# Layers 2 and 3 of a sparse graph stack: from a scheduler's order to one written by hand, with powers on GpSimd, W3 loaded in layer 1 and matrix products that nobody reads

## Chip, cores and metric

One core of one Trainium2 chip. The metric is the device time of one execution in microseconds: 997.93 us, the median of three runs (997.87 to 998.99). The profile comes from a fourth execution with the recorder on, which took 1028.73 us.

## What is computed

A stack of four graph layers on x (2708 nodes, 512 features, float32) with one weighted adjacency matrix adj (2708 x 2708, some 4 entries off the diagonal in a row). Each layer is added to its input and normalised over the features:

```python
x = ln(x + (x - (adj @ x) * (diag + 1)) @ weight + bias)                    # layer 0
# layer 1: h = x @ W_sa; attention e = exp(-leaky_relu(s_left + s_right)) where adj != 0
x = ln(x + sigmoid(gate_a * (e / e.sum(1)) @ h + gate_b * (adj @ (x @ W_gcnb) + b_gcnb)))
head = (adj > 0) / maximum(sqrt((adj > 0).sum(1)), 1e-12)                   # layer 2
inc = adj + head
x = ln(x + (inc @ x) / inc.sum(1))
A = adj + eye; d = A.sum(0) ** -0.5                                         # layer 3
x = ln(x + tanh((d[:, None] * A * d[None, :] @ x) @ W.T + b))
```

## The kernel before

**Blocks.** The rows are cut into NB = 24 blocks of R = 113 (the last has 109). In layer 0 each block's rows of adj are searched for their largest entries (`find`: `max` and `max_index` on four segments, L837 and L838), and the list of edges of a block is packed into EC = 4 chunks of 128. From there on a product with adj is sparse: `gather` (L613) fetches the source rows of a block's edges from a table in device memory with four indirect DMAs, issued by POOL, one per chunk of 128 rows; `values` (L1220) builds on DVE the 128 x 113 selection matrix of each chunk with the edges' values; `aggregate` (L626) multiplies the two on PE, eight passes of 128x512 a block (four products in float32, two passes each). There are NGB = 3 buffers for gathered rows, so gathers can run two blocks ahead. A gather for a layer can start only when all rows of its table have been stored (`move_rows`, L567, on SP's queue), since an edge may point to any row.

**Order.** Layers 0 and 1 are issued under a manual schedule (`by_hand`, entered at L656, closed after layer 1): the order of the code is the order on each engine. Layer 0 has a prologue (L1079 to L1160), in which the first blocks' searches, the loads of weights and the first products are interleaved by hand, and a loop over k = 1 to 23 (L1163), in which PE does for each block `o_l` (projection, L582), `h` and `hb` (the projections for layer 1) and `l0a` (aggregation). Layer 1's loop (L1465) has for each block the gathers of 4116-byte rows, two aggregations (`l1s`, `l1e`), the gates, a tanh, the statistics (`stats1`, whose add and power run on POOL, L1428 and L1429), and `norm1`, which stores the new x to table[1].

After the manual schedule is closed, the degrees go through device memory and back in another layout (L1501 to L1511), the row norms, row sums and d are computed for all blocks at once in [128 x 24] tiles (L1515 to L1547, square roots on ACT at L1523 and L1541), and layers 2 and 3 run through `run_layer` (L1234): for each block a gather two ahead, `prepare` one ahead, `compute`, and `finish` of the block before. Here a scheduler decides the order on each engine. Layer 2's `l2_prepare` turns the row norm into a row (`spread`: transpose on PE L1229, copy on ACT L1231) and makes the incidence (`inc`, L1564 and L1567, on DVE); at block 3 it issues the loads of b3 (to all 128 partitions) and W3 (1 MB). `l2_finish` has the node's own part on ACT (L1577), the sum on DVE (L1578), the `layernorm` (L591: statistics on DVE, square root on ACT L598, reciprocal and shift on DVE L599 and L601, scaling on ACT L604), and y = x d (L1583) to table[2]. Layer 3 aggregates again (`l3a`), adds the own part (`l3u`, L1599), transposes and projects with W3 (`tr_l` L573, `uT_l` L575, `o_l` L582), adds the bias (L1604), takes a tanh on ACT (L1607), adds x (L1608), normalises and stores.

The last lines of layer 1 and the two functions that set layers 2's and 3's order in the code are shown here with the rest that the diff touches.

Of the kernel before, what the change touches and what calls it, by code (L numbers as in the profile page):

```python
# [447 lines left out]
def sparse_stack(  # L448
# [142 lines left out]
    def layernorm(dst, v, r, name, scale=None, dst2=None):  # L591

        stats = small.tile([P, 6], FP, tag="stats", name=f"st_{name}")
        nc.vector.bn_stats(stats[:r, :], v)  # L594
        mv = small.tile([P, 2], FP, tag="mv", name=f"mv_{name}")
        nc.vector.bn_aggr(mv[:r, :], stats[:r, :])
        rstd = small.tile([P, 1], FP, tag="rstd", name=f"rs_{name}")
        nc.scalar.activation(rstd[:r, :], mv[:r, 1:2], AF.Sqrt, bias=eps_ln[:r, :])  # L598
        nc.vector.reciprocal(rstd[:r, :], rstd[:r, :])  # L599
        shift = small.tile([P, 1], FP, tag="shift", name=f"sh_{name}")  # L600
        nc.vector.tensor_scalar(  # L601
            shift[:r, :], mv[:r, 0:1], rstd[:r, :], -1.0, op0=ALU.mult, op1=ALU.mult
        )
        nc.scalar.activation(dst, v, AF.Identity, bias=shift[:r, :], scale=rstd[:r, :])  # L604

# [51 lines left out]
    with ExitStack() as phase:  # L657
# [117 lines left out]
        def spread_rows():  # L775
            for t in (ndiag, b0_bc):
                o = ps_o.tile([P, D], FP, tag="o", name="over_rows")
                nc.tensor.matmul(o, lhsT=one_row, rhs=t[0:1, :], start=True, stop=True)
                nc.scalar.copy(t, o)
            nc.vector.tensor_scalar(ndiag, ndiag, -1.0, -1.0, op0=ALU.mult, op1=ALU.add)  # L780
# [34 lines left out]

        def score_columns():
            w_a = work.tile([P, D], FP, tag="v", name="w_a_rows")
            nc.scalar.copy(w_a[0:2, :], w_saT["sum"][0:2, :])
            ps = ps_tr.tile([P, DB, P], FP, tag="tr", name="w_a_t")
            for f in range(DB):  # L820
                nc.tensor.transpose(ps[:, f, 0:2], w_a[0:2, f * P : (f + 1) * P], ident[0:2, 0:2])
            nc.scalar.copy(w_sa_sb[:, :, D : D + 2], ps[:, :, 0:2])
# [7 lines left out]
        def find(i, parts=range(NG)):  # L830

            a = abuf[i % NA]
            for g in parts:
# [3 lines left out]
                nc.vector.max(out=top, in_=seg)  # L837
                nc.vector.max_index(  # L838
                    out=where_all[:, i, g * 8 : (g + 1) * 8], in_max=top, in_values=seg
                )  # L840
# [237 lines left out]

        clear_diagonal(0)  # L1079
        negatives(0)  # L1080
        find(0)
        clear_diagonal(1)
        negatives(1)
        count(0)
        starts(0)
        find(1, (0,))
        ranges(0)
        nc.scalar.memzero(gflat[1])
        nc.scalar.memzero(gflat[2][:, KB * R + 3 * D :])
        mark(0)  # L1090
        fetch(0)
        find(1, (1,))
# [7 lines left out]
        w_gc_sb = load_w(w_gc, "w_gc_sb", first)  # L1100
        clear_diagonal(2)
        pick(0)
        values0(0)
        find(1, (2, 3))
        count(1)
        starts(1)
        find(2, (0,))
        ranges(1)
        negatives(2)
        mark(1)  # L1110
        spread_rows()
        fetch(1)
        find(2, (1,))
        clear_diagonal(3)
        pick(1)
        values0(1)

        nc.gpsimd.memset(abuf[4 % NA][:, NF, 0:1], 0.0)
        load_adj(4)
        sums0(0)  # L1120
        inputs0(0)
        turn_u(0)
        find(2, (2, 3))
# [4 lines left out]
        find(3, (0,))  # L1128
# [5 lines left out]
        fetch(2)  # L1134
        residual0(0)
# [6 lines left out]
        find(3, (1,))  # L1142
        norm0(0)
        values0(2)
# [3 lines left out]
        turn_u(1)  # L1148
        times_a(2)
        times_a(3)  # L1150
        score_columns()
        negatives(3)
        find(3, (2, 3))
        clear_diagonal(4)
        count(3)
        load_adj(6)
# [6 lines left out]
        for k in range(1, NB):  # L1163
            m, b = k + 2, k + 3
            if m < NB:
                starts(m)
                ranges(m)
            turn_x(k - 1)
            project0(k)
            if k > 1:  # L1170
                store0(k - 2)
# [3 lines left out]
            if m < NB:  # L1175
                mark(m)
                fetch(m)
# [3 lines left out]
            if b + 1 < NB:  # L1181
                clear_diagonal(b + 1)
            if m < NB:
# [3 lines left out]
            next0(k - 1)  # L1187
# [22 lines left out]
        rest0(NB - 1)  # L1210
        store0(NB - 1)
# [13 lines left out]

    def spread(col, name):

        ps = ps_s.tile([P, P], FP, tag="s", name=f"sp_{name}")
        nc.tensor.transpose(ps[:, :R], col[:R, :].to_broadcast([R, P]), ident[:R, :R])  # L1229
        row = spool.tile([P, R], FP, tag="row", name=f"row_{name}")  # L1230
        nc.scalar.copy(row, ps[:, :R])  # L1231
        return row

    def run_layer(src, n, prepare, compute, finish):  # L1234
        ahead = [gather(gath[i % NGB], i, src, n) for i in range(NGB - 1)]
        ready = prepare(0, ahead[0])
        done = None
        for i in range(NB):
            if i + NGB - 1 < NB:
                ahead.append(gather(gath[(i + NGB - 1) % NGB], i + NGB - 1, src, n))  # L1240
            ready_next = prepare(i + 1, ahead[i + 1]) if i + 1 < NB else None
            done_next = compute(i, ahead[i], ready)
            if i > 0:
                finish(i - 1, done)
            done, ready = done_next, ready_next
        finish(NB - 1, done)
# [202 lines left out]
    def spread_bias():  # L1449
        ps = ps_sp.tile([P, 4, P], FP, tag="sp", name="bg_rows")  # L1450
        ps = ps.rearrange("p k r -> p (k r)")
        nc.tensor.matmul(ps, lhsT=one_row, rhs=bg_bc[0:1, :], start=True, stop=True)
        nc.vector.tensor_copy(bg_bc, ps)
# [7 lines left out]
    spread_bias()  # L1461
    scores1(0)
    mask1(0)
    for i in range(NB):
# [9 lines left out]
        scored_sums1(i)  # L1474
        if i + 1 < NB:
# [9 lines left out]
        if i > 0:  # L1485
            norm1(i - 1)
        if i < KB:
            source_sum(i)
    both1(NB - 1)
    stats1(NB - 1)  # L1490
    norm1(NB - 1)
    phase.close()
    by_hand.close()

    ps_agg = ctx.enter_context(tc.tile_pool(name="ps_agg2", bufs=4, space=bass.MemoryType.PSUM))
    ps_tr = ctx.enter_context(tc.tile_pool(name="ps_tr2", bufs=1, space=bass.MemoryType.PSUM))
    ps_o = ctx.enter_context(tc.tile_pool(name="ps_o2", bufs=1, space=bass.MemoryType.PSUM))
    ps_s = ctx.enter_context(tc.tile_pool(name="ps_s2", bufs=2, space=bass.MemoryType.PSUM))


    deg_t = ps_s.tile([P, P], FP, tag="s", name="deg_t")  # L1501
    nc.tensor.transpose(deg_t[:KB, :], deg_k, ident)
    deg_c = gpool.tile([KB, P], FP, name="deg_c")
    nc.scalar.copy(deg_c, deg_t[:KB, :])
    nc.sync.dma_start(out=deg_d, in_=deg_c)
    flat_deg = deg_d.rearrange("b p -> (b p)")
    deg_r = gpool.tile([NB, R], FP, name="deg_r")
    nc.sync.dma_start(out=deg_r, in_=flat_deg[: NB * R].rearrange("(b p) -> b p", p=R))
    deg_s = ps_s.tile([P, P], FP, tag="s", name="deg_s")
    nc.tensor.transpose(deg_s[:R, :NB], deg_r, ident[:NB, :NB])  # L1510
    nc.scalar.copy(deg[:R, :], deg_s[:R, :NB])  # L1511

    plus = const.tile([P, NB], FP, name="plus")  # L1515
    nc.vector.tensor_scalar(plus, adiag, 0.0, None, op0=ALU.is_gt)
# [146 lines left out]
```

## Time and profile before

| What | Value |
|---|---|
| Median of three runs | 997.93 us |
| Profiled execution: time | 1028.73 us |
| Profiled execution: span from first to last instruction | 1026.9 us |
| Mean granted TensorE clock | 0.94 |
| PE busy in the span | 869.7 us (85%), 2921 instructions |
| DVE busy | 697.3 us (68%) |
| ACT busy | 598.6 us (58%) |
| POOL busy | 448.3 us (44%) |
| Moved by DMA | 190.80 MB, mean 186 GB/s |
| Layer 0 | 0 to about 428 us |
| Layer 1 (first `l1s` 442.7) | to about 650 us |
| Layer 2, first to last gather | 662.26 to 801.34 us |
| Layer 3, first gather to last product | 817.39 to 1012.7 us |

How to read it. Engines are PE (matrix products), PEld (loads of stationary operands, beside PE), DVE, ACT, POOL and SP (whose queue issues most plain DMAs). A group line names the source line, engine, operation, out<-in tiles and count, then the busy time and mean of one, and after the bar the engine's idle time before these instructions with what ended it: "<-issue" is time in which it waited for nothing that the profile shows, "<-remote" is a releaser that could not be placed. The granted clock is the share of full speed that PE's throttle allowed. The ends of matrix products are modelled in this recording, and single records can be missing.

### The profile page before, as it was taken

How to read it: one execution, taken by the hardware profiler on the slowest of the kernel's cores; microseconds unless marked ns; L12 is line 12 of the kernel's file. 1: busy time of each engine (PE TensorE's matmuls, PEld its weight loads, DVE VectorE, ACT ScalarE, POOL GpSimd, SP SyncE). 2: the span in 40 equal slices, each digit the busy share in tenths (PEclk: the TensorE clock that was granted, in tenths of full speed). 3: DMA queues.
4: the chain of work that ended last, by engine and by line, in shares of the span. 5: the costliest groups of instructions: out<-in, count | busy, mean ns of one | idle time of the engine just before them, and what ended most of it. 6: DMA issues, size and time to landing. Idle time of an engine off the chain costs nothing.

```text
span 1026.9 us, 11065 instructions
## 1 busy us (share of the span) xinstructions
PE 869.7 (85%) x2921; PEld 481.2 (47%) x2921; DVE 697.3 (68%) x1977; ACT 598.6 (58%) x1248; POOL 448.3 (44%) x492
## 2 busy tenths in 40 slices
PE   1889999999999999888888889386666568999993
PEld 1345555555555555456666667232222223444441
DVE  7778888888888873258887889645755515555553
ACT  7476676676666754357676766424433405666665
POOL 3222332323323221066666764276767275555510
PEclk9989999999999999989999999688889788999998
DMA  9856757657566334189999996276667364555521
GB/s 245 267 142 171 195 160 204 176 159 202 168 192 185 106 109 135 54 288 292 299 289 311 300 310 213 83 217 189 197 188 208 105 171 137 163 163 162 164 78 35
DMA packets 126857, 190.80 MB, mean 186 GB/s; under 512 B 81080, under 2 KB 81126, under 8 KB 126785
## 3 DMA queue, kind: packets, MB, share of 16 engines
q0 software_dynamic: 36864, 111.73, 36.5%
q1 hardware_dynamic: 89921, 78.28, 26.6%
q8 instruction: 25, 0.41, 0.2%
q14 instruction: 47, 0.39, 0.1%
HBM read 176.54 MB, written 27.80 MB: 199 GB/s over the span
## 4 chain that ended last, share of the span: by engine, by line
PE 60%; DVE 10%; DMA 10%; issue 6%; another core or an unknown queue 5%; ACT 4%; POOL 4%; SPq 0%; POOLq 0%; DVEq 0%; ACTq 0%
PE o_l L582 16%; DMA gath<-table,source 9%; PE h L582 8%; PE l0a L626 8%; PE hb L582 8%; PE l3a L626 7%; PE l2a L626 6%; POOL gath L613 3%; PE fetched L900 2%; PE tr_l L573 2%; ACT uT_l L575 1%; DVE st_l L1424 1%; DVE s L1220 1%; DVE e L1338 1%
## 5 line engine op out<-in xcount | busy, mean ns | idle before, releaser
L613 POOL DMA_INDIRECT gath<-table,source x288 | 311.3, 1081 | 200.4 <-issue 68.5
L613 POOL DMA_INDIRECT gath<-in_x_dram,source x96 | 96.8, 1008 | 261.3 <-issue 222.0
L626 PE MATMUL l2a<-gath,inc 128*113 128x512 f32 (+1 forms) x192 | 100.0, 673 | 48.7 <-DVE st_l L594 19.1
L1355 PE MATMUL l1s<-gath,s 128*113 128x256 f32 (+3 forms) x384 | 96.6, 407 | 26.9 <-DVE l1b L1385 26.4
L626 PE MATMUL l3a<-gath,s 128*113 128x512 f32 (+1 forms) x192 | 92.8, 607 | 11.4 <-DMA gath<-table,source 11.3
L582 PE MATMUL o_l<-shared,uT_l 128*113 128x512 f32 (+1 forms) x192 | 88.5, 604 | 11.3 <-issue 10.0
L1355 PEld LDWEIGHTS l1s<-gath,s 128*113 128x113 f32 (+1 forms) x384 | 70.3, 188 | 53.5 <-DVE l1b L1385 34.2
L582 PE MATMUL o_l<-w_sb,uT_l 128*113 128x512 f32 (+1 forms) x192 | 90.3, 614 | 2.2 <-ACT uT_l L575 1.1
L575 ACT COPY uT_l<-tr_l 128x452 f32<-128x452 f32 (+1 forms) x48 | 26.0, 541 | 112.3 <-PE tr_l L573 105.8
L582 PE MATMUL h<-w_sa_sb,uT_x 128*113 128x259 f32 (+1 forms) x384 | 88.3, 382 | 0.0
L626 PE MATMUL l0a<-gath,s 128*113 128x512 f32 (+1 forms) x192 | 88.2, 603 | 0.0
L1365 PE MATMUL l1e<-gath,e 128*113 128x257 f32 (+3 forms) x384 | 87.0, 379 | 0.0
L582 PE MATMUL hb<-w_gc_sb,uT_x 128*113 128x512 f32 (+1 forms) x192 | 86.6, 593 | 0.0
L626 PEld LDWEIGHTS l2a<-gath,inc 128*113 128x113 f32 (+1 forms) x192 | 36.6, 202 | 105.2 <-issue 65.7
L1365 PEld LDWEIGHTS l1e<-gath,e 128*113 128x113 f32 (+1 forms) x384 | 68.0, 177 | 15.5 <-issue 0.4
L582 PEld LDWEIGHTS h<-w_sa_sb,uT_x 128*113 128x113 f32 (+1 forms) x384 | 66.1, 177 | 15.2 <-issue 1.0
L582 PEld LDWEIGHTS o_l<-shared,uT_l 128*113 128x113 f32 (+1 forms) x192 | 32.7, 180 | 62.4 <-issue 49.2
L1599 DVE SCALAR_TENSOR_TENSOR l3u<-xr,dself,l3a 113x512 f32<-113x512 f32 (+1 forms) x24 | 17.9, 747 | 60.9 <-PE l3a L626 52.7
L1220 DVE TENSOR_SCALAR s<-niota_r,nrow,edges 128x113 f32<-128x113 f32 x192 | 58.8, 336 | 0.4 <-PE l1s L1355 0.4
L626 PEld LDWEIGHTS l3a<-gath,s 128*113 128x113 f32 (+1 forms) x192 | 32.8, 182 | 51.4 <-issue 36.5
L582 PEld LDWEIGHTS hb<-w_gc_sb,uT_x 128*113 128x113 f32 (+1 forms) x192 | 33.9, 177 | 46.5 <-issue 46.0
L582 PEld LDWEIGHTS o_l<-w_sb,uT_l 128*113 128x113 f32 (+1 forms) x192 | 32.9, 181 | 44.6 <-issue 37.5
(240 smaller groups left out, 1591.5 us busy)
## 6 DMA issues: line engine op xcount, KB each, us to landing
shared<-in_adj_dram SPq DMA_DIRECT2D x14, 1186.5 KB
table<-st SPq DMA_DIRECT2D x23, 450.2 KB
shared<-table SPq DMA_DIRECT2D x23, 448.0 KB
gath<-in_adj_dram SPq DMA_DIRECT2D x7, 1186.5 KB
xi<-in_x_dram SPq DMA_DIRECT2D x23, 224.0 KB
table<-xr SPq DMA_DIRECT2D x23, 224.0 KB
table<-y SPq DMA_DIRECT2D x23, 224.0 KB
out_dram<-y SPq DMA_DIRECT2D x23, 224.0 KB
```

The source lines that it names most:

```text
L573: nc.tensor.transpose(tr[:, f, :r], u[:r, f * P : (f + 1) * P], ident[:r, :r])
L575: nc.scalar.copy(uT[:, :, :r], tr[:, :, :r])
L582: nc.tensor.matmul(o, lhsT=uT[:, f, :r], rhs=w[:, f, :], start=(f == 0), stop=(f == DB - 1))
L613: nc.gpsimd.indirect_dma_start(out=g[:, c, :n], out_offset=None, in_=src[:, :], in_offset=bass.IndirectOffsetOnAxis(ap=source[:, i, c : c ...
L626: nc.tensor.matmul(agg[:r, :], lhsT=s[:, c, :r], rhs=g[:, c, off : off + D], start=(c == 0), stop=(c == EC - 1),)
L900: nc.tensor.matmul(t["fetched"][:, c, : 3 * NS], lhsT=t["q"][:, c * P : (c + 1) * P], rhs=rec_all[:, i].rearrange("p k s -> p (k s)"), sta ...
L1220: nc.vector.tensor_scalar(s[:, c, :], niota_r, nrow[:, i, c : c + 1], edges[:, i, c, 1:2], op0=ALU.is_equal, op1=ALU.mult,)
L1338: nc.vector.tensor_tensor(e, gath[i % NGB][:, :, SR : SR + 1].to_broadcast([P, EC, R]), over_chunks(s_left[:, i, :]), ALU.add,)
L1355: nc.tensor.matmul(sum_s[i][:r, k, : at.stop - at.start], lhsT=s[:, c, :r], rhs=g[:, c, at], start=(c == 0), stop=(c == EC - 1),)
L1365: nc.tensor.matmul(sum_e[i][:r, k, k : k + at.stop - at.start], lhsT=e[:, c, :r], rhs=g[:, c, at], start=(c == 0), stop=(c == EC - 1),)
L1424: nc.vector.bn_stats(stats[:r, :], v[:r, :])
L1599: nc.vector.scalar_tensor_tensor(u[:r, :], x3, dself[:r, i : i + 1], agg[:r, :], op0=ALU.mult, op1=ALU.add)
```

## The change

The manual schedule is no longer closed after layer 1 but at the end of the kernel. `run_layer`, `layernorm` and `spread` are gone, and layers 2 and 3 are written out in the order in which each engine is to do them. The main parts:

1. **Layer 0's prologue** is reordered: searches split into values and places, `negatives`, `clear_diagonal` and the zeroing of buffers moved later, `values0` of blocks 1 and 2 behind their neighbours' turns, the score columns split and moved into k = 1. `keep_busy(n)` issues n matrix products of 128x512 into a PSUM tile that is never read: 6 at the start, then 2, 1, and 4 ahead of layer 0's last store.
2. **Layer 1's last blocks** now hold the degrees' way out (block 22) and back (block 23), the row norms for columns 0 to 21 (block 22) and 22 to 23 (after the loop), as maximum on DVE and a power on POOL in place of square root and reciprocal, and the loads of b3 (one row, spread by a product and a copy on DVE) and W3, after block 22's norm. d is a power on POOL too. Twelve unread products (`keep_warm`) stand between the last block's products and b3's spreading.
3. **Layer 2**: turning and copying the norm two blocks ahead, the copy first on ACT; the aggregation; one unread product a block; the statistics of the block before; values two ahead; and so on, as below. The incidence has a ring of three places in memory that layer 1 used for s_left. The last two `values` of the loop are those of layer 3's blocks 0 and 1. Nine unread products follow the loop.
4. **Layer 3**: the projection is one block behind the aggregation, the tanh and the norm two behind; the statistics take add and power on POOL in place of the square root on ACT. The last block's tanh and statistics go by halves of 256 columns.

PSUM for layers 2 and 3 is laid out anew: two buffers for aggregations (four before), two for projections (one before), two for turned rows, one for transposes, one for unread products.

```diff
+        def keep_busy(n):
+
+            o = ps_o.tile([P, D], FP, tag="o", name="unread")
+            for _ in range(n):
+                nc.tensor.matmul(o, lhsT=ident, rhs=iota_t, start=True, stop=True)
...
+        keep_busy(6)
         clear_diagonal(0)
         negatives(0)
         find(0)
...
+        keep_busy(1)
         inputs0(0)
         turn_u(0)
+        values0(1)
         find(2, (2, 3))
...
-        values0(2)
         inputs0(1)
         times_a(1)
         turn_w(3)
         turn_u(1)
+        values0(2)
         times_a(2)
         times_a(3)
-        score_columns()
-        negatives(3)
-        find(3, (2, 3))
+        score_rows()
+        find(3, (1, 2, 3))
...
         for k in range(1, NB):
             m, b = k + 2, k + 3
+            if k == 1:
+                turn_x(k - 1)
+                project0(k)
             if m < NB:
                 starts(m)
+                if k == 1:
+                    score_columns()
                 ranges(m)
...
+    def keep_warm(pool, tag, shape, n, cols=D):
...
+        for _ in range(n):
+            nc.tensor.matmul(o[:, :cols], lhsT=ident, rhs=bg_bc[:, :cols], start=True, stop=True)
...
+    def row_norms(at):
...
+        nc.vector.tensor_scalar(inv_norm[:, at], cnt[:, at], 1e-24, None, op0=ALU.max)
+        nc.gpsimd.tensor_tensor(
+            inv_norm[:, at], inv_norm[:, at], root.to_broadcast([P, n]), ALU.pow
+        )
...
         scored_sums1(i)
+        if i + 1 == NB:
+            source_sums_in()
+            turn_norm(0)
+            turn_norm(1)
...
             norm1(i - 1)
+        if i + 1 == NB:
+            nc.sync.dma_start(out=b3_bc[0:1, :], in_=b3[None, :])
+            nc.sync.dma_start(out=w3_sb, in_=w3T.rearrange("(b p) o -> p b o", p=P))
         if i < KB:
             source_sum(i)
+        if i == KB:
+            source_sums_out()
+            row_norms(slice(0, KB))
+    row_norms(slice(KB, NB))
+    copy_norm(0)
+    copy_norm(1)
+    keep_warm(ps_sp, "sp", [P, 4, P], 12)
     both1(NB - 1)
     stats1(NB - 1)
-    norm1(NB - 1)
-    phase.close()
-    by_hand.close()
...
-    nc.scalar.activation(inv_norm, inv_norm, AF.Sqrt)
-    nc.vector.reciprocal(inv_norm, inv_norm)
...
+    norm1(NB - 1)
...
-    nc.scalar.activation(d_inv, d_inv, AF.Sqrt)
-    nc.vector.reciprocal(d_inv, d_inv)
+    nc.gpsimd.tensor_tensor(d_inv, d_inv, root.to_broadcast([P, NB]), ALU.pow)
+    spread_bias(b3_bc)
+    phase.close()
...
+    own2(0)
+    for i in range(NB):
+        if i + 2 < NB:
+            gather(gath[(i + 2) % NGB], i + 2, table[1], D)
+            turn_norm(i + 2)
+            copy_norm(i + 2)
+        sum2[i] = aggregate(inc2.pop(i), gath[i % NGB], rows(i), f"l2a{i}")
+        if i + 1 < NB:
+            keep_warm(ps_u, "u", [P, D], 1)
+        if i > 0:
+            stats2(i - 1)
+        s = values((i + 2) % NB)
+        if i > 0:
+            norm2(i - 1)
+        if i + 1 < NB:
+            own2(i + 1)
+        if i + 2 < NB:
+            incidence(i + 2, s)
+        else:
+            edge_3[(i + 2) % NB] = s
+    stats2(NB - 1)
+    norm2(NB - 1)
...
+    keep_warm(ps_u, "u", [P, D], 9)
...
+        nc.gpsimd.tensor_scalar(mv[:r, 1:2], mv[:r, 1:2], 1e-5, None, op0=ALU.add)
+        nc.gpsimd.tensor_tensor(mv[:r, 2:3], mv[:r, 1:2], root[:r, :], ALU.pow)
...
+    for i in range(2):
+        gather(gath[i], i, table[2], D)
...
+    for i in range(NB + 1):
+        if i + 2 < NB:
+            gather(gath[(i + 2) % NGB], i + 2, table[2], D)
+        if i > 0:
+            uT = turned(u3.pop(i - 1), rows(i - 1), f"l3_{i - 1}")
+        if i < NB:
+            sum3[i] = aggregate(edge_3.pop(i), gath[i % NGB], rows(i), f"l3a{i}")
+        if i > 1:
+            tanh3(i - 2, whole)
+        if i + 2 < NB:
+            edge_3[i + 2] = values(i + 2)
+        if i > 0:
+            project3(i - 1, uT)
+        if i > 1:
+            stats3(i - 2, whole)
+        if i < NB:
+            inputs3(i)
+        if i > 1:
+            norm3(i - 2)
+    tanh3(NB - 1, two)
+    stats3(NB - 1, two)
+    norm3(NB - 1)
+    by_hand.close()
```

## Prediction

> **What bounds the kernel now.** I read the windows by stage first, then the groups, the waits of the gathering engine, and the chain across the joint of layers 2 and 3.
>
> ```profile
> 430.00:650.00 220.00, 187.09 (x799) 142.70 (x797) 175.06 (x453) 144.31 (x361) 132.44 (x142) 0.95 0.86 273
> 650.00:662.00 12.00, 2.17 (x6) 0.99 (x6) 10.09 (x42) 9.19 (x15) 1.17 (x2) 0.56 0.13 39
> 662.00:815.00 153.00, 100.77 (x210) 39.03 (x210) 85.04 (x253) 59.71 (x114) 97.71 (x96) 0.82 0.64 190
> 815.00:850.00 35.00, 18.66 (x43) 7.15 (x43) 6.54 (x15) 3.08 (x5) 24.26 (x24) 0.75 0.57 158
> 850.00:1012.00 162.00, 160.75 (x437) 68.83 (x438) 85.84 (x229) 107.58 (x133) 75.36 (x73) 0.99 0.46 137
> ```
>
> Columns: stretch and length, then busy PE, PEld, DVE, ACT, POOL, then granted clock, DMA share, GB/s. Layer 1 (430 to 650) lives on its transfers (share 0.86) and is hardly touched. Layer 3 from 850 on is PE-bound: 160.75 of 162 us. Between lie three stretches where no engine is full, at clocks of 0.56, 0.82 and 0.75.
>
> ```profile
> L613 POOL DMA_INDIRECT gath<-table,source x96 | 97.7, 1018 | 45.6 <-issue 19.8 <-remote 12.5 <-PE l2a L626 5.5
> L1578 DVE SCALAR_TENSOR_TENSOR l2v<-l2a,row_cnt,l2v 113x512 f32<-113x512 f32 (+1 forms) x24 | 18.0, 748 | 34.3 <-remote 26.0 <-PE l2a L626 6.4 <-issue 1.8
> POOL gath L613 <- DMA table<-y: 16.0, 1, 16.0
> ```
>
> A gather takes 1.02 us and about 0.29 us of issue follows, so 1.306 us each and 5.22 us a block. That is layer 2's floor: 24 x 5.22 = 125.4 us. It took 139.1 us (662.26 to 801.34): 13.7 us too long. After the last gather another 16.0 us pass before layer 3's first gather.
>
> ```profile
> 819.99 3.70 DMA gath<-table,source
> 829.12 1.10 PE l3a L626 x2
> 833.19 8.35 another core or an unknown queue
> 841.60 6.31 another core or an unknown queue
> 847.93 0.76 DVE l3u L1599
> 849.95 5.12 PE o_l L582 x8
> ```
>
> On one core "another core" cannot be meant. DVE and ACT wait there for PE's semaphore: between 831.8 and 841.5 ten passes of 128x512 took 9.7 us, where the warm L0 loop needs 0.43 each. Such joint stalls of 7 to 10 us come at 688, 714, 744, 784 and 833; a granted clock of 0.5 over 10.2 us follows each. I read them as PE running at half clock after idle stretches.
>
> ```profile
> L582 PE MATMUL o_l<-shared,uT_l 128*113 128x512 f32 (+1 forms) x183 | 84.5, 605 | 11.3 <-issue 10.0 <-ACT uT_l L575 1.2
> L598 ACT ACT_TABLE_LOAD x23 | 29.5, 1283 | 0.4
> L1607 ACT ACT_TABLE_LOAD x22 | 28.2, 1283 | 27.8 <-DVE l3v L1604 26.4 <-issue 1.4
> ```
>
> In layer 3 o_l's first start is 849.95 and its last 1009.02: 159.1/22 = 7.23 us a block. The 45 table loads (57.7 us of ACT) are beside that PE work and cost nothing, except at the end.
>
> ```profile
> 56.92 1.27 PE w_a L810 x2
> 58.22 0.58 ACT w_a_rows L818
> 58.85 0.58 PE w_a_t L821 x4
> 60.80 5.28 PE o_l L582 x8
> 66.95 3.51 PE h L582 x16
> 70.47 3.43 PE l0a L626 x8
> ```
>
> This is the chain into the L0 loop. From o_l at 78.37 on, PE takes 15.95 us a block without a hole, so what is won before it is kept.
>
> **What the Trainium skill says.** "TensorE: Matmul & The Clock Gate", What's actually happening: the array falls to half its clock after an idle window of about 3.4 us of a free-running counter, and needs a busy one to come back. The trace agrees in kind (eight passes 5.3 to 5.5 us cold, 3.5 to 3.7 warm; clock 0.5 for 10.2 us at a time). "ScalarE: Activation LUTs", Table sets: square root and tanh are of different sets, so alternating them loads a table each time; the trace has two loads a block, 1.283 us each. "GPSIMD Engine Reference", Elementwise: about 2.6 cycles per element for two inputs; no price for a power. The trace has one only at [113,1]: 0.57 us, against 0.22 for a simple scalar operation. "DMA: Bandwidth & Descriptors", Issuing engines are not separate DMA queues: queues of all engines share the same 16 DMA engines; the trace agrees: W3 and b3 (1.25 MB), issued at 661, share 662 to 669 with layer 2's first gathers, and l2a starts at 669.68.
>
> **Part by part**, in the profiled execution's own time (1028.73 us; span 1026.9, 1.8 around it). It is 30.8 us longer than the median of 997.93.
>
> *L0's prologue.* The six unread products at the start have PE to themselves. score_columns goes behind project0(1): 1.27 + 0.58 + 0.58 = 2.4 us leave the chain. values0(2), four ACT selections of 0.48 us ahead of uT's copy, goes behind turn_u: 1.9 us. o_l(1) warm instead of cold: 5.28 - 3.69 = 1.6 us. Sum -5.9. Next in line is DVE with the split searches (0.66 to 0.94 us an instruction, none removed). From -2 to -9; I take -6. The four products before the last store0 fill the hole at 428 to 442: -0.5.
>
> *Joint of layers 1 and 2.* Two square roots and their loads leave ACT: table loads at 651.46 and 654.93, and tanh's own switch at 652.99; 2 x 1.28 = 2.6 us. Against that, source_sums_in's ACT copy stands ahead of the last block's gates, waiting for PE: I take +2 us. W3 and b3 (now one row) are issued under layer 1's block 23, some 9 us earlier: 1.25 MB at the 300 GB/s of layer 1 is 4.2 us of its transfers, of which block 23's gathers are already in. First gather about 662 as now. First l2a: twelve unread products, 12 x 0.43 = 5.2 us warm or 10.3 cold, then b3's copy: about 667.5. POOL goes on meanwhile as there are three buffers, so the gain here is 0, -3 to +5. The degrees' round trip (two small DMAs on SP's queue, behind layer 1's last stores) now starts a block earlier, with the 8 us of block 23 beside its two landings of some 2 us: nothing. On that queue W3 stands ahead of xr's last store, but 9 us before it. Powers: one column is between 0.02 us (the page's rate, an estimate) and 0.35 us (0.57 - 0.22); 24 columns 1 to 8.5 us, I take 4. That for columns 0 to 22 has an 8 us block beside it. d_inv's stands on POOL ahead of layer 2's first gather; its cover is the store's landing (658.0 to 662.26, 4.2 us); at 8.5 it costs 4.3.
>
> *Layer 2.* Per block: PE 8 x 0.43 + 0.26 + one unread 0.43 = 4.1 us; DVE 85.0/24 = 3.5; ACT 59.7/24 = 2.5; all under POOL's 5.22. turn_norm and copy_norm two blocks ahead, and the copy first on ACT, break the ring l2a, inc, row_in that turned one late block into a stall. ACT's square root waits on DVE as now, with own2 and the next copy_norm behind it; these have a block of slack. PE is asked for 4.1 of 5.22 us, no idle window, so it stays warm. Of 13.7 us I give 3 back for stalls that I don't see: -11.
>
> *Joint of layers 2 and 3.* Now 801.34 to 817.39, in which l2a ends 8.7 us after the last gather. With PE one block behind: last gather landed and used after 3.2, statistics and norm 4, landing of y 3.3: 10.5 us. -5.5. Nine unread products (3.9 warm, 7.8 cold) lie wholly in this gap.
>
> *Layer 3.* Now first l3a 820.8 to last o_l 1012.7: 191.9. PE warm: 24 x 7.23 = 173.5, plus gathers setting the pace of the first three blocks, 3 x (5.22 - 3.46) = 5: 178.5. -13. The 45 loads become one; POOL takes add and power, 0.22 + 0.57 us ahead of gathers, with 7.23 - 5.22 = 2.0 us spare. *Tail:* no load, halves: -1.5.
>
> Sum: -6 - 0.5 + 0 - 11 - 5.5 - 13 - 1.5 = -37.5, so 991.2 us profiled. Times 997.93/1028.73 = 0.970: 961.5. I say **962**.
>
> **Rivals.** *A: the joint stalls are mostly an effect of recording.* The profiled run is 30.8 us longer, and records are missing where PE stalls end (o_l at 849.95 shows 3 of 8 passes); but the clock column is low there too. Then the unprofiled layer 2 is already near its floor: of 11 + 13 remain perhaps 4: -37.5 + 20 = -17.5, **981**. *B: layer 2 in its fixed order gets another bound*: each DVE wait on l2a now holds the next incidence, and each ACT wait the next own2. One exposed semaphore chain of the length of sh to xr (0.6 us) in each block gives 24 x 0.6 = 14: **976**. *C: slower.* One unread product makes PE's block 4.1 us of full clock. Where the granted clock falls under 4.1/5.22 = 0.79, PE sets layer 2's pace (now 0.82 on the mean of the stage). At half clock a block is 8.2 us, 3.0 over POOL's: 24 x 3.0 = 72, with layer 2's 11 lost: 962 + 83 = **1045**. Against it: PE would have to stay cold while 80% busy, and L0's loop shows 1.00. *D: the prologue gains nothing*, because DVE's searches set it: **968**, inside the forecast's range.
>
> **How the numbers follow.** Forecast with D: 0.60 (948 to 972); A 0.20 (974 to 988); B 0.10 (970 to 982); C 0.04; 0.06 that more is won than I see (under 948: first gathers of layer 2 earlier by the 4.2 us of landing, unread products helping layer 1's end). Range 946 to 986: it leaves out C, most of the last case, and the ends of A. A measurement here tells 0.2% (2 us) from no change. Faster by more: 0.60 + 0.20 + 0.10 + 0.06, less 0.02 that I take off A for an end at no change: 0.94. Within: these 0.02. Slower: C's 0.04.
>
> **What would show it.** Right, in the changed profile: no joint stalls of 7 us and PEclk 9 or more through layer 2; gathers of layer 2 within 129 us first to last; the wait on table<-y near 10 us; layer 3 at 7.2 us a block from its second block on; 5 table loads in all; o_l(2) near 72 us instead of 78. Wrong: a clock of 0.5 with PE busy in layer 2 (C), DVE or ACT ending POOL's waits (B), stalls vanished in the profile and a smaller gain without it (A), a power over 5 us on POOL before the first gather.

## The result

The changed kernel takes 993.63 us (median of 9 runs, 991.35 to 996.93), the kernel before 998.69 us beside it (997.31 to 1000.11): a ratio of 0.9958, 95% interval 0.9944 to 0.9973. That is 5 us faster, where 36 were forecast (997.93 to 962). The forecast of 962 and its range of 946 to 986 both miss.

The profiled execution of the changed kernel took 996.16 us (span 994.3), inside its timed runs. That of the kernel before had taken 1028.73, outside all of its own: against that one recording the change looks 32.6 us faster, and 27 of these are not there when the two are timed. This is what the study had to explain.

The same stretches as before, now of the changed kernel (columns: stretch and length, then busy PE, PEld, DVE, ACT and POOL, granted clock, DMA share, GB/s):

```profile
430.00:650.00 220.00, 187.47 (x805) 142.07 (x804) 175.93 (x452) 144.41 (x364) 136.94 (x144) 0.96 0.86 272
650.00:662.00 12.00, 12.00 (x24) 4.95 (x23) 2.66 (x13) 0.81 (x1) 8.35 (x7) 0.82 0.47 147
662.00:815.00 153.00, 134.89 (x305) 49.97 (x304) 105.44 (x289) 65.88 (x120) 109.68 (x106) 0.97 0.68 196
815.00:850.00 35.00, 35.00 (x98) 15.35 (x97) 19.89 (x49) 9.65 (x15) 28.03 (x32) 1.00 0.64 178
```

The clock stands at 0.97 and 1.00 where it stood at 0.82 and 0.75, PE is busy throughout, and POOL's idle time ahead of its gathers has fallen from 200.4 to 139.7 us. First before, then changed:

```profile
L613 POOL DMA_INDIRECT gath<-table,source x288 | 311.3, 1081 | 200.4 <-issue 68.5
L598 POOL DMA_INDIRECT gath<-table,source x288 | 314.9, 1093 | 139.7 <-issue 66.7
```

Read alone, that is the forecast come true. The trap is the other half of the comparison.

### The profile page after: what moved, and what is told of

Read it like the earlier page. It is cut to its first block, busy times and chain, and to the rows that moved or that the text cites. A ratio compares the mean times of both kernels' runs of the same rounds, so it can differ in the third digit from the quotient of the medians.

```text
span 994.3 us, 11251 instructions
## 1 busy us (share of the span) xinstructions
PE 913.7 (92%) x3037; PEld 496.8 (50%) x3037; DVE 709.1 (71%) x1956; ACT 528.3 (53%) x1174; POOL 480.1 (48%) x543
## 5 line engine op out<-in xcount | busy, mean ns | idle before, releaser
L598 POOL DMA_INDIRECT gath<-table,source x288 | 314.9, 1093 | 139.7 <-issue 66.7
L1347 PE MATMUL l1s<-gath,s 128*113 128x256 f32 (+3 forms) x384 | 94.6, 401 | 26.8 <-DVE l1b L1377 26.6
L611 PE MATMUL l2a<-gath,s_left 128*113 128x512 f32 (+1 forms) x192 | 96.5, 623 | 13.0 <-DMA gath<-table,source 10.2
L611 PE MATMUL l3a<-gath,s 128*113 128x512 f32 (+1 forms) x192 | 88.5, 603 | 3.5 <-DMA gath<-table,source 3.5
L582 PE MATMUL o_l<-shared,uT_l 128*113 128x512 f32 (+1 forms) x192 | 86.5, 593 | 0.6 <-ACT uT_l L575 0.6
L1705 ACT ACTIVATE y<-l3v,mv_l 113x512 f32<-113x512 f32 (+1 forms) x24 | 19.5, 813 | 88.0 <-DVE mv_l L1701 83.5
L611 PEld LDWEIGHTS l2a<-gath,s_left 128*113 128x113 f32 (+1 forms) x192 | 30.6, 182 | 68.6 <-DMA gath<-table,source 40.7
L611 PEld LDWEIGHTS l0a<-gath,s 128*113 128x113 f32 (+1 forms) x192 | 34.2, 179 | 38.4 <-issue 36.7
```

Of the source, the lines that this page charges most:

```text
L582: nc.tensor.matmul(o, lhsT=uT[:, f, :r], rhs=w[:, f, :], start=(f == 0), stop=(f == DB - 1))
L598: nc.gpsimd.indirect_dma_start(out=g[:, c, :n], out_offset=None, in_=src[:, :], in_offset=bass.IndirectOffsetOnAxis(ap=source[:, i, c : c ...
L611: nc.tensor.matmul(agg[:r, :], lhsT=s[:, c, :r], rhs=g[:, c, off : off + D], start=(c == 0), stop=(c == EC - 1),)
L1347: nc.tensor.matmul(sum_s[i][:r, k, : at.stop - at.start], lhsT=s[:, c, :r], rhs=g[:, c, at], start=(c == 0), stop=(c == EC - 1),)
L1705: nc.scalar.activation(y[:r, :], v[:r, :], AF.Identity, bias=mv[:r, 3:4], scale=mv[:r, 2:3])
```

## Experiments

Theory S at the outset: the joint stalls of layers 2 and 3 exist only where a recording is made, and the change has taken away something that the timed runs of before never had. Rivals: they come by chance (T), or they are in every execution and the change gives the time back elsewhere (H). Eighteen kernels ran in five groups, each group on one chip, and each on another. A "stall" or "hold-up" here is a stretch in which PE starts nothing and the other engines wait for its results.

### First group: the kernel before again, and parts of the change

x1 is the kernel before, unchanged.

> The kernel before, unchanged, recorded a second time. Theory S (the joint stalls of layers 2 and 3 exist only in a recorded execution): the recorded execution again takes 15 to 45 us more than the timed ones, and the excess lies in stalls of several us between 662 and 850; the timed runs stay at 998 +- 1. Rival T (the stalls come by chance in any execution, the first recording was an outlier): the recording takes about 998 to 1003 and shows no such stalls; then layer 2's and 3's milestones of this recording are within 3 us of those of the changed kernel, moved by what comes before them. Rival H (stalls are in every execution): recording at 1028 and the timed runs would have to hold the same stalls, so a granted clock of about 0.94 in the timed runs too.

x2 has the change's layer 0 (part 1 of the change) and nothing else of it.

> The kernel before with the change's layer 0 alone (prologue, loop at k = 1, the unread products of layer 0). Theory S: the prologue's part, read from the traces as 3.1 us at the second block's own part and 3.2 at layer 1's first product, is most of the whole gain of 5 us: 994.5 to 996 us. Rival (the prologue gain is eaten by layer 1, which is bound by transfers): 997.5 to 998.7, and the gain of the change lies behind layer 1.

x3 is the changed kernel without the unread products of layers 1 to 3:

```diff
-    keep_warm(ps_sp, "sp", [P, 4, P], 12)
...
-        if i + 1 < NB:
-            keep_warm(ps_u, "u", [P, D], 1)
...
-    keep_warm(ps_u, "u", [P, D], 9)
```

> The changed kernel without the 43 unread products of layers 1 to 3 (12 ahead of layer 2, one in each block of layer 2 but the last, 9 behind it); layer 0's stay. Theory S: gathers set layer 2's pace and the unread products neither help nor hurt by more than 3 us; 992 to 997. Rival H (they keep the clock up and so save the stalls): 1005 to 1030 timed, with a granted clock under 0.95. Rival U (they are on the path at the joints): 988 to 991.

x4 is the changed kernel with all of layer 0 as before.

> The changed kernel with the layer 0 of before. Theory S: it loses the prologue's 3 us and keeps 1 to 2 from the joint of layers 1 and 2: 996 to 997.5. Rival (all the gain is in layers 1 to 3): 993 to 994.5.

| Kernel | Median, us | Ratio to before (1021.22, 49 runs) |
|---|---|---|
| x1, before again | 1021.39 | 1.0002 (0.9981 to 1.0023) |
| x2, layer 0 alone | 1017.21 | 0.9966 (0.9944 to 0.9988) |
| x3, no unread products | 1003.85 | 0.9859 (0.9808 to 0.9910) |
| x4, layer 0 of before | 1013.67 | 0.9916 (0.9893 to 0.9939) |

x3's six executions fall into two clusters, four at 1002.4 to 1004.9 us and two at 1014.2 and 1014.3.

None of the theories had expected the first line: the kernel before itself now takes 1012 to 1029 us in every execution, timed or recorded. The recorded execution is not set apart from the timed ones (x1's, 1017.52, lies among 1015.71 to 1024.89), so S falls, and with it the reason that the prediction's rival A gave. H falls too: there are executions at 998. Something that holds for the whole group of runs decides. And x4 shows that the stalls stay in the hand-written order, with PE full of products. Its PE around 692 us (start, length, instructions, idle before them):

```profile
692.35 0.26 PE L1465 MATMUL sp_in<-ident,inv_norm 113*128 113x113 f32 x1
692.45 3.60 PE L611 MATMUL l2a<-gath,s_left 128*113 128x512 f32 x8
701.31 2.07 PE L1441 MATMUL unread<-bg_bc,ident 128*128 128x512 f32 x2 [5.27 <-remote]
703.18 0.40 PE L1465 MATMUL sp_in<-ident,inv_norm 113*128 113x113 f32 x1
```

and DVE, which waits for the sum:

```profile
694.33 0.63 DVE L1481 TENSOR_TENSOR s_left<-s_left,s 128x452 f32<-128x452 f32 x1
701.25 0.75 DVE L1582 SCALAR_TENSOR_TENSOR l2v<-l2a,row_cnt,l2v 113x512 f32<-113x512 f32 x1 [6.29 <-remote]
```

Eight passes start at their full 0.43 us, the last at 695.45, then nothing starts for 5.3 us. The unread product waits for no other engine, only for PE's own signal of the sum before it, and DVE waits for the same one: both go on at 701.25 to 701.31. The two passes after it take 1.03 us each, and the clock record has 0.5 from 698.3 for 6.8 us. The half clock follows the hold-up; it isn't its start.

Whether PE itself stood still or only its signals came late isn't shown. The recordings with hold-ups hold fewer of PE's signals than others: between 662 and 800 us, 70 in the first recording and 84 in x1, against 114 in y1 below, the same kernel. In layer 0 (60 to 430 us), where no time is lost, it is 223 and 225 against 249. So a stretch without a signal measures nothing by itself; the waits do. In the five recordings with hold-ups and unread products in layer 2 (x4, w1, w2, w3, u1), PE's wait ahead of such a product is 1.7 to 6.8 us, three to five times in layer 2 (waits under 1.5 us left out).

### Second group: a chip without hold-ups

> The kernel before once more, in another call. In the call before, every execution of it took 1012 to 1029 us, where the first timed runs took 997 to 1000. Theory C (the chip decides: on some chips PE is held up for about 3.5 us and then runs at half clock for 7 to 10 us, several times in layers 2 and 3; on others it isn't): the runs of this call are either all near 998 with no such stall in the recording, or all near 1020 with 4 to 6 of them. Rival R (recording or the moment decides, not the chip): times from 998 to 1025 mixed within this call.

> The changed kernel once more. Theory C: on a chip without the stalls 993 to 994, 5 us under before; on one with them about 1009 (the earlier 1013.7 with layer 0 of before, less the prologue's 4), 11 to 13 us under before. Rival (the changed order does away with the stalls wherever it runs): 992 to 996 on any chip.

> The kernel before with the change's layer 0 alone. In the call before it was 4.0 us faster. Theory C: layer 0 shows none of the stalls, so the same 3 to 4.5 us on any chip: on one without stalls 994 to 995, which leaves 0.5 to 1.5 us for all of layers 1 to 3.

> The changed kernel without the 43 unread products of layers 1 to 3. Theory C: on a chip without stalls they are beside the gathers and cost or win at most 2 us, 992 to 995; on one with stalls they add to PE's load and it is 5 us or more faster without them (1003.9 in the call before). Rival H (they keep the clock up): slower than the changed kernel by over 3 us on a chip without stalls.

y1 is before, y2 the changed kernel, y3 and y4 are x2 and x3 again.

| Kernel | Median, us | Ratio to before (999.33, 38 runs) |
|---|---|---|
| y1, before | 999.55 | 0.9998 (0.9982 to 1.0015) |
| y2, changed | 993.61 | 0.9938 (0.9917 to 0.9959) |
| y3, layer 0 alone | 996.35 | 0.9973 (0.9964 to 0.9983) |
| y4, no unread products | 993.68 | 0.9952 (0.9934 to 0.9970) |

Theory C (its words stand at y1) foresaw this: all runs of before lie between 995.9 and 1003.3, and no group of the study mixes, for this kernel, such times with those over 1012. But no chip was met twice, so the chip and the moment can't be told apart, and nothing is on record of what the chip's other cores did. Nor does the record name the chip of the first recording: if it was that of the three timed runs at 998, something else than the chip changed. The recording y1 is the one that the prediction would have needed, layers 2 and 3 of the kernel before with no hold-up in them:

```profile
662.00:815.00 153.00, 109.49 (x233) 37.13 (x234) 87.84 (x262) 61.39 (x116) 108.60 (x107) 0.92 0.69 205
815.00:850.00 35.00, 35.00 (x95) 14.80 (x94) 17.21 (x47) 20.46 (x26) 25.75 (x25) 1.00 0.68 196
```

POOL's waits there (total, times, longest) know no "remote", and table<-y holds it for 12.4 us instead of 16.0:

```profile
POOL gath L613 <- issue: 17.7, 58, 0.3
POOL gath L613 <- DMA table<-y: 12.4, 1, 12.4
```

The stages of three recordings, each from the start of a stage's first gather to the next mark:

| Stage, us | First recording of before | y1, before | y2, changed |
|---|---|---|---|
| Layer 0, to its last own part (`l0u` of block 23) | 408.0 | 407.8 | 405.5 |
| from there to layer 1's first gather | 27.9 | 28.2 | 27.8 |
| Layer 1, first gather to block 23's | 188.9 | 187.1 | 189.4 |
| to layer 2's first gather | 37.5 | 36.6 | 36.2 |
| Layer 2, first gather to block 23's | 132.4 | 122.5 | 124.3 |
| to layer 3's first gather | 22.8 | 17.3 | 16.8 |
| Layer 3, first gather to block 23's `l3u` | 186.0 | 174.3 | 174.2 |
| from there to the end | 23.6 | 23.4 | 21.0 |

Between the first two columns, the same kernel, lie 9.9 + 5.5 + 11.7 = 27.1 us in layers 2 and 3. The change has nearly nothing there: + 1.8 - 0.5 - 0.1. Layer 1 is bound by its transfers, and its 23 blocks take 185.0 to 189.6 us over all twenty recordings, with hold-ups in layers 2 and 3 or without, which speaks against slower transfers as their cause; y2 lies near the upper end, and its recorded execution (997.0) is the slowest of its runs.

### Third group: single steps and a combination

w1 takes layer 3's root back to ACT:

```diff
-        nc.gpsimd.tensor_scalar(mv[:r, 1:2], mv[:r, 1:2], 1e-5, None, op0=ALU.add)
-        nc.gpsimd.tensor_tensor(mv[:r, 2:3], mv[:r, 1:2], root[:r, :], ALU.pow)
+        nc.scalar.activation(mv[:r, 2:3], mv[:r, 1:2], AF.Sqrt, bias=eps_ln[:r, :])
+        nc.vector.reciprocal(mv[:r, 2:3], mv[:r, 2:3])
```

> The changed kernel with layer 3's square root back on ACT (square root and reciprocal in stats3, in place of add and power on POOL), so two table loads in each block of layer 3 again, in the hand order. The prediction's step (loads lie beside PE's work and cost only at the end): 1 to 2.5 us slower than the changed kernel, all of it after the last l3u, and l3u's pace unchanged at 7.2 us. Rival (the loads hold up DVE's in-order queue and with it the next l3u): the pace rises by 0.2 us or more, 5 us slower or worse. Times hold for a chip without stalls (changed kernel 993.6).

w2 takes d_inv's root back to ACT, behind layer 1's last norm:

```diff
-    nc.gpsimd.tensor_tensor(d_inv, d_inv, root.to_broadcast([P, NB]), ALU.pow)
+    nc.scalar.activation(d_inv, d_inv, AF.Sqrt)
+    nc.vector.reciprocal(d_inv, d_inv)
```

> The changed kernel with d_inv's root on ACT and a reciprocal on DVE, in place of the power on POOL (4.17 us on 24 columns), which in the recordings ends 0.17 us before layer 2's first gather starts. If the power sets that gather: first gather 1.0 to 1.3 us earlier against the last norm of layer 1, time 992.5 on a chip without stalls. If the landing of the last store sets it: no difference within 0.3 us there.

w3 has four more unread products in layer 0:

```diff
+                if k == 1:
+                    keep_busy(4)
                 turn_u(k + 1)
```

> The changed kernel with four more unread products in layer 0, at k = 1 ahead of turn_u(2), where PE waits 2.3 us for DVE and the eight o_l passes that follow take 5.38 us instead of 3.6. If cold passes are the price of that hole: o_l at 3.6 to 4 us, 1.5 us faster. If the unread products only push the transposes back (four of 0.43 to 0.86 us are 1.7 to 3.4 in a hole of 2.3): no gain, up to 1 us slower. Nothing either way if DVE sets the block behind it.

w4 is w2 and w3 together, less the unread products of layers 1 to 3.

> The changed kernel with d_inv's root on ACT, the four unread products at k = 1, and none of the 43 unread products of layers 1 to 3. On a chip without stalls 991 to 992.5 by the sum of the parts (-1.1, -1.5, 0); on one with stalls 8 us or more under the changed kernel, since PE's load in layers 2 and 3 is less.

This chip had hold-ups: before 1024.68 us (15 runs), w1 1015.12, w2 1010.00, w3 1011.40, w4 1008.91 (ratios 0.9911, 0.9874, 0.9892 and 0.9867, intervals 0.6 to 0.9% wide). The intervals overlap, so the sums decide nothing between the four; the recordings answer each question at its place.

*w1.* Forty table loads are back between 847 and 994 us, 51.4 us of ACT:

```profile
L1683 ACT ACT_TABLE_LOAD x20 | 25.7, 1283 | 0.3
L1694 ACT ACT_TABLE_LOAD x20 | 25.7, 1283 | 0.4
```

and l3u's pace over its last 19 steps is 7.25 us, as in w2 (7.26). The end takes 21.2 us from the last l3u, against 20.6 to 20.9 in w2, w3 and w4. So the loads cost the pace nothing. At the end they show 0.3 to 0.6 us against these three, not the 1 to 2.5 expected, and even that can't be told from none: the recordings with the power on POOL there take 20.6 to 21.3 us.

*w2.* In y2 the power of 24 columns occupies POOL up to layer 2's first gather:

```profile
652.98 0.56 POOL L1421 TENSOR_TENSOR mv_l<-mv_l,root 109x1 f32<-109x1 f32 x1
654.60 4.17 POOL L1578 TENSOR_TENSOR d_inv<-d_inv,root 128x24 f32<-128x24 f32 x1 [1.06 <-DVE d_inv L1577]
658.94 1.17 POOL L598 DMA_INDIRECT gath<-table,source  x1 [0.17 <-issue]
```

In w2 it is gone, and the gather starts 3.37 us after the end of the last norm (651.16), where in y2 it is 4.30 us (654.64): 0.9 us, near the 1.0 to 1.3 expected. It repeats: from the end of POOL's last power on one column to the gather it is 5.40 us in every recording with d_inv's power on POOL and 4.46 in all three of the changed order without it (w2, w4, v2).

```profile
649.50 0.56 POOL L1421 TENSOR_TENSOR mv_l<-mv_l,root 109x1 f32<-109x1 f32 x1
654.53 1.17 POOL L598 DMA_INDIRECT gath<-table,source  x1 [4.46 <-issue]
```

*w3.* In y2, behind the prologue, PE waits for DVE and runs the next projection cold:

```profile
67.00 3.60 PE L582 MATMUL hb<-w_gc_sb,uT_x 128*113 128x512 f32 x8
72.88 0.58 PE L573 MATMUL tr_l<-ident,l0u 113*128 113x113 f32 x4 [2.28 <-DVE l0u L963]
73.29 0.29 PE L873 MATMUL fetched<-totals,under 128*128 128x1 f32 x2
73.45 0.58 PE L573 MATMUL tr_x<-ident,xr 113*128 113x113 f32 x4
74.09 5.38 PE L582 MATMUL o_l<-w_sb,uT_l 128*113 128x512 f32 x8
```

In w3:

```profile
69.76 3.60 PE L770 MATMUL unread<-gath,ident 128*128 128x512 f32 x8
73.20 0.55 PE L573 MATMUL tr_l<-ident,l0u 113*128 113x113 f32 x4
...
74.38 3.69 PE L582 MATMUL o_l<-w_sb,uT_l 128*113 128x512 f32 x8
```

The four products are eight passes, 3.4 us: the hole is overfilled, yet o_l is warm at 3.69 and done at 78.07 instead of 79.47. This pair alone misleads, though, since the recordings start their count at different moments, and since chance has a part: without the four products, o_l of block 2 is cold in nine of the thirteen recordings of this layer 0 and warm in four (x2, y4, v1, u2). Counted from the start of o_l of block 1 to the last own part, layer 0 takes 351.2 to 351.3 us in the nine, 349.6 in the four, and 350.6 with the four products (w3, w4). So the cold passes cost 1.7 us, and four unread products win back 0.7 of it where they meet them and lose 1.0 where they don't.

### Fourth and fifth group: a full PE against a half empty one

v1 has two unread products in each block of layer 2 instead of one. v4 has about half of PE's work there (it leaves most of the sums of 256 columns out):

```diff
-        sum2[i] = aggregate(inc2.pop(i), gath[i % NGB], rows(i), f"l2a{i}")
-        if i + 1 < NB:
-            keep_warm(ps_u, "u", [P, D], 1)
...
+        for c in range(EC):
+            nc.tensor.matmul(
+                agg[:r2, :H], lhsT=s2[:, c, :r2], rhs=g2[:, c, :H],
+                start=(c == 0), stop=(c == EC - 1),
+            )
+        nc.tensor.matmul(
+            agg[:r2, H:], lhsT=s2[:, EC - 1, :r2], rhs=g2[:, EC - 1, H:D], start=True, stop=True
+        )
```

v2 is w4 with two unread products at k = 1 instead of four, v3 the changed kernel once more.

> The changed kernel with two unread products in each block of layer 2 instead of one. Each is two passes of 0.43 us, so PE's block is 8 x 0.43 + 0.26 + 1.72 = 5.4 us, over POOL's 5.22. On a chip without stalls: PE sets the pace, 23 x 0.2 = 4 to 6 us slower than the changed kernel. On a chip with stalls: if alternation brings them on, a full PE has none in layer 2 and its gathers take about 126 to 129 us there, less than 131; if load brings them on, they stay or come more often, 135 us or more.

> The changed kernel with d_inv's root on ACT, two unread products (four passes, 1.7 us in a hole of 2.3) at k = 1, and none of the 44 unread products of layers 1 to 3 (counted as 43 before). On a chip without stalls 991 to 992.5, 1 to 2.5 under the changed kernel; on one with stalls 3 us or more under it.

> The changed kernel once more, for comparison on the same chip. Theory C: 993 to 994 on a chip without stalls, 1008 to 1013 on one with them, where before takes 1021 to 1025.

> The changed kernel with layer 2's sums cut: over all four chunks only for the first 256 columns, over the last chunk alone for the other 256, and no unread product in layer 2's blocks (so the output of layer 2 is left incomplete, all else is done). PE's block falls from 4.6 to about 2.4 us. On a chip without stalls: layer 2's gathers keep their 5.3 us a block, time as the changed kernel within 2 us. On a chip with stalls: if load brings them on, they are gone from layer 2 and its gathers take 122 to 126 us; if alternation brings them on, they stay, 130 us or more.

The chip had no hold-ups: before 998.59 us (11 runs), v1 992.73 (0.9943, 0.9921 to 0.9965), v2 993.88 (0.9941, 0.9921 to 0.9960), v3 994.35 (0.9953, 0.9935 to 0.9970), v4 992.56 (0.9940, 0.9918 to 0.9962). No difference among the four can be told. v1 was to be 4 to 6 us slower and isn't: PE is busy for 123.00 of the 123 us from 662 to 785, and layer 2's gathers take 121.9 us. Its block of PE comes to 5.25 us (l2a starts at 668.34 and at 673.59), not to 5.4. That is POOL's own pace of 5.22, so a PE clearly slower than the gathers was not tried. v2, the combination of what looked good, gains nothing that can be told: o_l of block 2 is warm in it (3.69 us, and 349.6 us to the last own part), but layer 3 took 176.2 us in its recording, 2 us more than in the others. v4 with half the work has the same 124.3 us: gathers set layer 2, not PE. The last group, u1 and u2, is v1 and v4 again.

> The changed kernel with two unread products in each block of layer 2, on another chip if it comes so. On a chip without stalls as measured before: 993, before 998.6. On a chip with stalls (before over 1012): if alternation of idle and busy stretches brings them on, layer 2's gathers take 122 to 127 us; if load does, 131 us or more.

> The changed kernel with layer 2's sums cut to some half of PE's work (256 columns over four chunks, the other 256 over the last chunk alone) and no unread product in its blocks. On a chip without stalls as measured before: 992.6. On a chip with stalls: if load brings them on, layer 2's gathers take 122 to 126 us; if alternation does, 130 us or more.

Now the chip had hold-ups: before 1025.21 us (5 runs), u1 1013.99 (0.9898, 0.9823 to 0.9974), u2 1013.73 (0.9886, 0.9814 to 0.9958). Layer 2's gathers took 132.8 and 133.0 us, as in every recording with hold-ups (130.6 to 132.8 in the nine others of the study). A full PE doesn't avoid them, and one half empty isn't spared. u1 at 736 us:

```profile
735.55 1.02 PE L611 MATMUL l2a<-gath,s_left 128*113 128x512 f32 x2
739.30 3.68 PE L1470 MATMUL unread<-bg_bc,ident 128*128 128x512 f32 x4 [2.73 <-remote]
```

u2 at 721 us:

```profile
720.93 0.59 PE L1649 MATMUL l2a<-gath,s_left 128*113 128x256 f32 x2
721.36 0.26 PE L1494 MATMUL sp_in<-ident,inv_norm 113*128 113x113 f32 x1
730.34 2.90 PE L1645 MATMUL l2a<-gath,s_left 128*113 128x256 f32 x6 [8.72 <-DVE l2v L1611]
```

Both explanations fall, as far as PE's work in layer 2 goes: load (u2 was to take 122 to 126 us) and alternation (u1 was to take 122 to 127). In layer 3 the hold-ups come in the first blocks alone: `l3u`'s pace over the last 19 steps is 7.22 to 7.28 us in all twenty recordings.

## Why the prediction was wrong

**The step that failed** is the one line that took the profile's sum over to the median: "Times 997.93/1028.73 = 0.970". It spread the recording's 30.8 us of excess evenly over the kernel. In fact 27.1 of them lay in the hold-ups of layers 2 and 3, and these were what the three largest terms (-11, -5.5, -13) promised to win. Three timed runs within 1.1 us of each other, 30 us under the recording, could not have held them. The prediction had the number and the stalls side by side; rival A said so with a chance of 0.20, and its sign, stalls gone from the profile and a smaller gain without it, is the one that came; but its reason (recording) was wrong, and it kept 17.5 us of gain where there were 5.

**Half clock after idle stretches.** I read the stalls as PE cooling off. The Trainium skill, "TensorE: Matmul & The Clock Gate", What's actually happening, does describe half clock after an idle window, and the trace shows it after true pauses: in y4, without unread products, the record has 0.5 for 17.1 us at the joint of layers 1 and 2, for 10.2 at that of 2 and 3, and the time is that of y2 (993.68 and 993.61). But a hold-up comes with PE full (u1) as well, and the first recording spoke against this reading already:

```profile
838.92 1.02 PE L626 MATMUL l3a<-gath,s 128*113 128x512 f32 x2
849.95 2.90 PE L582 MATMUL o_l<-shared,uT_l 128*113 128x512 f32 x3 [10.01 <-issue]
```

The passes before run at 0.43 us each (eight of o_l in 3.62 us at 832.50), then nothing starts for 10 us, and the clock record goes to 0.5 only within that stretch, from 842.6. "Ten passes took 9.7 us" was the distance of two signals, not the passes' time. The "3 of 8 passes" of rival A were no missing records: the window asked for ended at 852, and the chain in the prediction lists all eight.

What causes the hold-ups stays open. Shown is that they hold for a whole group of runs or are absent from it, and that neither the hand-written order nor the unread products nor PE's load in layer 2 does away with them.

**Layer 0: -6 forecast.** Layer 0's end came 2.3 us earlier in y2, and layer 0 alone gave 0.9973 of 999.33, 2.7 us. Up to o_l of block 1 the sum was right: it starts at 54.21 us instead of 60.78 (y1), 6.6 earlier and warm. But its own block then takes 19.9 us to o_l of block 2, where it took 17.4: the score columns' transposes come back in it, and PE waits 2.28 us for DVE. So o_l of block 2 started at 74.09, not 72; it had started at 78.13. Of these 4.0 us, another 1.7 went in its own cold passes (5.38 against 3.69). The prediction named DVE as the next in line and then took the whole 5.9. The -0.5 of the four products ahead of the last store is not there: from the last own part to layer 1's first gather it is 27.8 to 28.0 us with them, and 27.8 to 28.2 without (first recording, x1, x4, y1).

**Joint of layers 1 and 2: 0 forecast,** and none that can be told: 36.2 to 36.8 us in three recordings of the changed kernel, 36.6 to 37.5 in three of before. The power of 24 columns took 4.17 us, against 4 estimated, and ends 0.17 us before the gather; 0.9 of it is exposed. (The prediction's lower price of a column, 0.02 us, doesn't follow from the rate that it cites, which gives about a tenth of that.) W3's early load is not to be seen in the time.

**Layer 2: -11.** Without hold-ups before needs 122.5 us for 23 blocks, 5.33 each, where 23 x 5.22 = 120.1 is the floor that the prediction itself had worked out. Only 2.4 us could be won; the change's recordings show 124.3 to 124.8. To call PE's block 4.1 us was an error besides: an unread product in float32 is two passes, 0.86 us, so 4.6; the twelve and the nine were priced at half for the same reason. Rival C's slower end didn't come: v1 adds a further 0.86, just fills PE, and costs nothing.

**Joint of layers 2 and 3: -5.5; layer 3: -13.** -0.5 and -0.1. Layer 3 is 24 blocks of PE's 7.28 us before and 7.26 after. That loads of tables are free beside PE was right (w1).

**The end: -1.5.** -2.4, all from the last l3u on, and it repeats: 23.3 to 23.6 us in the five recordings with this part as before, 20.6 to 21.3 in the fifteen others. What the loads have of it doesn't stand clear of the scatter (w1); halves and order were not taken apart.

On chips with hold-ups the changed kernel itself wasn't run; two variants with one small step altered (w2, w3) stand at 0.987 and 0.989 of before, 11 to 13 us. Where the larger gain lies there is open. It isn't in layer 2, whose gathers take 130.9 to 132.4 us in the old order and 130.6 to 133.0 in the new. Whether the unread products cost time there is open too: x3 stands under x4 by 10 us, of which layer 0 explains some 4, but w4 does not stand clear of w2 and w3. And recordings of one kernel differ by 11 us (before: 1015.7 and 1026.9).

## What to carry to other kernels

Before any stall is priced, compare the recorded execution's time with the timed runs: if it lies outside them by as much as the stalls amount to, the stalls are not in the time that is to be shortened, and a second recording costs less than a plan built on the first. Then set each stage against its own floor (gathers, passes) and against the timed total; what a floor leaves over is the most that an order can win, here 2.4 us in layer 2, where 11 were promised.

## What the runs showed of the hardware

- In three of the five groups of runs, each on its own chip, every execution was longer: 1012 to 1029 us for the kernel before, against 996 to 1003 in the other two. The recordings there show PE starting nothing for 1.7 to 6.8 us, three to five times in layer 2, while it waits for no engine but itself, mostly with half clock for 3.4 to 10.2 us after it. Layer 0's loop, with PE full for 362 to 364 of 366 us, shows none.
- A power on POOL took 0.57 us for one column, 0.70 for two, 3.86 for 22 and 4.17 for 24: about 0.16 us a column and 0.4 fixed.
- Eight passes of 128x512 took 5.38 us cold and 3.69 warm. Whether one place in layer 0 was cold differed between recordings of the same kernel (cold in y3 and u1, warm in x2 and v1).
- Unread products shortened the half clock at the joints (from 17.1 to 13.6 us and from 10.2 to 3.4, y4 against y2), and that was worth nothing without hold-ups, since gathers and landings end those waits.
